# A causal cross-attention and expert layer on one core: the order of the attention step, with one slot of single products per step instead of two

## The chip, the core and the metric

The kernel runs on one core of one Trainium2 chip. A core has a matrix engine (TensorE, PE in the profile; its weight loads are the row PEld), a vector engine (VectorE, DVE), a scalar engine (ScalarE, ACT), a general engine (GpSimd, POOL) and a queue that issues transfers (SyncE, SP). Each engine works through its own list of instructions in order and waits on semaphores that the others raise. Products land in PSUM, from where DVE and ACT read them; everything else is in SBUF or in HBM (DRAM).

The metric is the time of one execution in microseconds (us) of device time, lower is better. Where several runs were taken, their median is given.

## The reference

Everything is float32. Four sequences of 1024 tokens with 512 features pass through an attention layer and a layer of experts, both with a residual.

```python
# attention, 16 heads of 32
qh, kh = (ln(x) @ Wq.T), (ctx @ Wk.T)          # by head
vh = ctx @ Wv.T + bv
scores = einsum('bhsd,bhtd->bhst', qh, kh) / sqrt(32)
mask = triu(ones((1024, 1024)), k=0); mask[0, 0] = False
probs = softmax(where(mask, -inf, scores))
x = x + (einsum('bhst,bhtd->bhsd', probs, vh)) @ Wo.T + bo
# experts: in each group of 32 tokens every one of 128 experts takes the token with its largest logit
perm = (logits == max over the 32 tokens of logits)
x = x + combine(relu(dispatch(ln(x), perm) @ f1 + bias) @ f2, perm)
```

Row s of the scores uses keys before s only (row 0 its own key), so about half of every 1024x1024 block is computed. The attention is what the change is about; the routing and expert phases come after it and their code is not touched.

## The kernel before, in words

**Units and steps.** The attention is cut into 16 units: 4 sequences times 4 chunks of four heads. A unit has 12 steps (k = 0 to 11), and every engine's list is written out by hand in the order of the Python loop (only the transfers on SP are placed by the scheduler of the framework).

In a step of unit u, three attention products are made, each for four heads at once:

- `score_piece(u+1, k)` makes row-major scores of the *next* unit: 128 queries against up to 512 keys (L401, four matmuls that use 32 rows of the array each and run side by side), for 8 of the 12 steps followed by a product that adds the causal mask (L407, full array). DVE takes the row maxima from PSUM, one instruction for two heads (L413). The widths for k = 0 to 11 are 128, 256, 384, 512, 512, 128, 512, 256, 512, 384, 512, 512; pieces 4, 6, 8 and 10 have no mask.
- `key_block(u, k)` makes key-major scores of *this* unit: 128 keys against up to 512 queries (L467), and subtracts the row maxima, which were made one unit before, by a second product (L473). ACT takes the exponential from PSUM (L481), and POOL zeroes the masked part on the diagonal (L484). The widths are 512, 384, 256, 128, 512, 512, 512, 512, 512, 384, 256, 128.
- `weigh_values(u, k)` multiplies the exponentials of block k with the values (L517, four matmuls that use 32 columns of the array each, side by side). It is put on a list, `pending`, and made when the list holds LAG = 2, so two steps after its block.

The sums of the exponentials are added up by POOL and DVE (L500 to L504); at the end of each half of a unit `normalize` makes their totals on PE (L543), takes reciprocals and multiplies the result (L538).

**Three PSUM buffers for two kinds of scores.** Pieces and blocks take two buffers each from one pool of three (`ps_s`, each of two banks). Since they alternate, the first half of a block takes the buffer that the block before had for its second half, and the second half takes the one that the piece before had for its first half; pieces likewise. So a block's second half can't start before DVE has read the first half of the piece ahead of it, and a piece's second half not before ACT has read the first half of the block ahead of it.

**Single products.** Between these come the products that prepare later units or finish earlier ones: queries (L288), keys (L274), values (L307), output rows (L348), and the small turn of the row maxima (L439, "pmx"). They use the full array and one PSUM bank (`ps_m`), so a second one waits until ACT or DVE has emptied the bank of the first. They stand in lists (`fill`, `soon`), and `slot(slots_left, until)` takes from them: it works towards a backlog that falls evenly over the slots left, and further while the planner's clock `now` is before `until`. `ensure` forces those that are needed next. A product is cut into four parts of one 512-wide matmul (a value product into four of four 128-wide ones), so a slot can stop in the middle.

**The planner's clock.** `now`, `dve`, `act` and `bank` hold the author's estimates of when each engine is done; `scores_free()` says when both halves of the next pair of score buffers are free. These estimates decide the order only; nothing of them is in the program.

Before the change, a step reads (L716 to L763): piece; a slot until the score buffers are free; the value product if they are still not free; block; sums; the value product if it was not made; a second slot.

Of the kernel before, what the change touches and what calls it, by code (L numbers as in the profile page):

```python
# [37 lines left out]
def attention_phase(  # L38
# [20 lines left out]
    NU = B * NC  # L59

    LARGE, SMALL, TURN = 0.86, 0.11, 0.2
    now, dve, act, bank = [0.0], [0.0], [0.0], [0.0]

    read = deque([0.0] * 3)
# [5 lines left out]
    def scores_free():  # L72
        return max(read[0], read[1]) + 0.1

    def scores_given(work, engine, cost):
        now[0] = max(now[0], scores_free()) + work
        for _ in range(2):
            read.popleft()
            read.append(given(engine, cost))
# [308 lines left out]
    def score_piece(u, k):  # L388
        i, c0, n = pieces[k]
        kT, qT = ks[u], qs[u]  # L390
        half = i // 4
        if (u, half) not in nms:
            nms[u, half] = spool.tile([P, 2, 4, R], F32, tag=f"nm{half}", name=f"nm_{u}_{half}")
        nm = nms[u, half]
        scs = [
            ps_s.tile([P, 2, HS], F32, tag="sc", name=f"sc_{u}_{k}_{g}") for g in range(2)
        ]
        diag = c0 + n == (i + 1) * P
        for r in range(R):
            rr = ds(r * HD, HD)  # L400
            nc.tensor.matmul(  # L401
                scs[r // 2][:, r % 2, :n], lhsT=qT[rr, ts(i, P)], rhs=kT[rr, ds(c0, n)],
                start=True, stop=not diag,
            )
        if diag:
            for r in range(R):
                nc.tensor.matmul(  # L407
                    scs[r // 2][:, r % 2, ds(n - P, P)], lhsT=ident16,
                    rhs=masks[0 if i == 0 else 1], start=False, stop=True,
                )  # L410
        scores_given(LARGE * n / HS + (0.45 if diag else 0.1), dve, 0.15 + 2.1e-3 * n)
        for g in range(2):
            nc.vector.tensor_reduce(  # L413
                nm[:, c0 // HS, i % 4, ts(g, 2)], scs[g][:, :, :n], AX.X, ALU.max, negate=True
            )
# [166 lines left out]

    fill, soon, done = deque(), deque(), set()
    open_step, backlog = [None], [0.0]
    RESERVE = 5.0
# [20 lines left out]
    def choose(force):  # L608
        for i in range(len(soon)):
            if soon[i][0] <= now[0] or (force and not fill):  # L610
                step = soon[i][1]
                del soon[i]
                return step
        return fill.popleft() if fill else None

    def slot(slots_left, until=0.0):

        goal = backlog[0] - max(0.0, backlog[0] - RESERVE) / slots_left
        if backlog[0] > goal or now[0] < until:
            now[0] += TURN  # L620
        while backlog[0] > goal or now[0] < until:
            if open_step[0] is None:
                if now[0] < bank[0]:
                    return
                open_step[0] = choose(False)
                if open_step[0] is None:
                    return
            if not advance(open_step[0]):
                open_step[0] = None
# [20 lines left out]
    def ensure(*names):  # L650
        while not done.issuperset(names):
            one_part()
# [27 lines left out]
    def o_todo(b, t0, t1):  # L680
        return [o_step(b, t, ahead=(b, t + 1) if t + 1 < NT else None) for t in range(t0, t1)]
# [5 lines left out]
    STEPS = len(blocks)  # L687
    LAG = 2
    pending, sums = deque(), deque()
    for half in range(2):  # L690
        done.update((kind, 0, half) for kind in "qkv")
    for u in range(-1, NU):
        b, hc = divmod(u, NC)
        q_todo, k_todo = kq_steps(u + 2) if u + 2 < NU else ([], [])
        v_todo = v_steps(u + 1) if 0 < u + 1 < NU else []
        more = 0 <= b < B - 1

        rows, r0 = [], 0
        if b > 0:
            if hc == 0:  # L700
                load_residual(b - 1, 0)
            ends = (3, 6, 8, 8) if more else (2, 4, 7, 8)
            r0 = ends[hc - 1] if hc else 0
            rows = o_todo(b - 1, r0, ends[hc])
        if more and hc == 0:
            ln_rows(b + 1)
        add("q", u + 2, q_todo[:1] if more and hc == 2 else q_todo)
        if more and hc == 1:
            load_ctx(b + 1, 0)
            add("t", b + 1, [ln_step_turned(b + 1)], 0.0)  # L710
        add("v", u + 1, v_todo)
        if more and hc == 2:
            add("c", b + 1, [load_step(b + 1, 1)], 0.0)
            add("k", u + 2, k_todo[:1])
            add("o", b - 1, rows, first=r0)
            add("k", u + 2, k_todo[1:], first=1)  # L716
            add("q", u + 2, q_todo[1:], first=1)
        else:
            add("k", u + 2, k_todo)
            add("o", b - 1, rows, first=r0)  # L720
        for k in range(STEPS):
            if u + 1 < NU:
                if k in (0, 4):
                    ensure(("q", u + 1, k // 4), ("k", u + 1, k // 4))
                score_piece(u + 1, k)
                if k == 4:
                    split_maxima(u + 1, 0)
                if k == STEPS - 1:
                    split_maxima(u + 1, 1)
            weighed = False  # L730
            slot(2 * (STEPS - k), scores_free() if u >= 0 else 0.0)
            if u >= 0 and len(pending) == LAG and now[0] < scores_free():
                pending.popleft()()
                weighed = True
            if u >= 0:
                h, j = blocks[k]
                finish(("split", u, h, 0), ("split", u, h, 1))
                while (u, h) not in mxTs:
                    one_part()
                key_block(u, k)  # L740
            if sums:
                sums.popleft()()
            beside(0.9)
            if len(pending) == LAG and not weighed:
                pending.popleft()()
            if u >= 0:

                def add_first(u=u, k=k):
                    add_sums(u, k, 0, nc.vector)

                def weigh(u=u, k=k):
                    h, j = blocks[k]
                    ensure(("v", u, j // 4))
                    weigh_values(u, k)
                    if j == 4 * (h + 1) - 1:
                        if h == 0 and NC <= u and u % NC == NC - 1:
                            ensure(("o", u // NC - 1, NT - 1))
                        soon.append((now[0], normalize(u, h)))

                add_sums(u, k, 1, nc.gpsimd)  # L760
                sums.append(add_first)
                pending.append(weigh)
            slot(2 * (STEPS - k) - 1, scores_free() if u + 1 < NU else 0.0)  # L763
    while sums:
        sums.popleft()()
    while pending:
# [396 lines left out]
```

## Time and profile before

| | us |
|---|---|
| median of 3 runs | 1498.17 |
| runs | 1489.71, 1498.17, 1499.57 |
| the profiled execution's own time | 1487.66 |
| its span, from first to last instruction | 1485.9 |
| PE busy in the span | 1400.1 |
| DVE busy | 926.8 |
| ACT busy | 502.7 |
| POOL busy | 486.4 |
| mean granted clock of PE | 0.972 of full |

The profile shows one execution. A group of instructions is named by its line in the kernel, its engine, and `out<-in` by tile names: `sc` is a piece of row-major scores, `st` a block of key-major scores, `av` the value product, `pr` the exponentials, `pq`, `pk`, `pv`, `po` the single products. A float32 matmul makes two passes through the array, and each pass is one record: a group of four matmuls shows as x8. Ends of matmuls are modelled, starts are recorded, so what a group takes is read here from its start to the start of the next group. The attention steps fill the span from 39.9 us (first piece) to 1138.3 us (last value product); the routing and expert phases follow.

### The profile page before, as it was taken

How to read it: one execution, taken by the hardware profiler on the slowest of the kernel's cores; microseconds unless marked ns; L12 is line 12 of the kernel's file. 1: busy time of each engine (PE TensorE's matmuls, PEld its weight loads, DVE VectorE, ACT ScalarE, POOL GpSimd, SP SyncE). 2: the span in 40 equal slices, each digit the busy share in tenths (PEclk: the TensorE clock that was granted, in tenths of full speed). 3: DMA queues.
4: the chain of work that ended last, by engine and by line, in shares of the span. 5: the costliest groups of instructions: out<-in, count | busy, mean ns of one | idle time of the engine just before them, and what ended most of it. 6: DMA issues, size and time to landing. Idle time of an engine off the chain costs nothing.

```text
span 1485.9 us, 31726 instructions
## 1 busy us (share of the span) xinstructions
PE 1400.1 (94%) x13704; PEld 739.5 (50%) x13704; DVE 926.8 (62%) x1377; ACT 502.7 (34%) x785; POOL 486.4 (33%) x557
## 2 busy tenths in 40 slices
PE   6999999999899999999999999999997988968996
PEld 4344544354344534443434344444533547868886
DVE  3666777565657676666767755655754554756664
ACT  1033333423232233232323233232333124636662
POOL 1034334343334343435253443434366200000212
PEclk9999999999999999999999999999997996988999
DMA  8011201002231300012211100010113788652654
GB/s 298 21 50 32 76 24 66 20 1 59 38 111 36 96 29 19 10 52 47 72 60 50 33 11 10 10 38 19 38 47 122 268 273 241 191 193 79 207 181 143
DMA packets 96972, 125.25 MB, mean 84 GB/s; under 512 B 12992, under 2 KB 54336, under 8 KB 96704
## 3 DMA queue, kind: packets, MB, share of 16 engines
q1 hardware_dynamic: 94272, 114.84, 24.9%
q0 software_dynamic: 2560, 8.39, 1.9%
q8 instruction: 107, 1.75, 0.5%
q14 instruction: 33, 0.27, 0.1%
HBM read 91.78 MB, written 31.42 MB: 83 GB/s over the span
## 4 chain that ended last, share of the span: by engine, by line
PE 78%; issue 7%; DVE 5%; DMA 5%; POOL 2%; ACT 1%; SPq 0%; POOLq 0%; DVEq 0%; ACTq 0%
PE sc L401 12%; PE st L467 10%; PE av L517 8%; PE pq L288 8%; PE pk L274 8%; PE pv L307 8%; PE po L348 5%; PE pd L957 3%; PE sc L407 3%; DVE nm L413 2%; PE pi L976 2%; PE st L473 2%; PE po L808 2%; PE pl L845 2%; PE pd L543 2%
## 5 line engine op out<-in xcount | busy, mean ns | idle before, releaser
L413 DVE TENSOR_REDUCE nm<-sc 128x2 f32<-128x1024 f32 (+3 forms) x384 | 349.1, 951 | 265.3 <-PE sc L407 178.9
L481 ACT ACTIVATE pr<-st 128x1024 f32<-128x1024 f32 (+3 forms) x384 | 290.4, 808 | 583.9 <-PE st L473 557.6
L484 POOL TENSOR_SCALAR_AFFINE_SELECT pr<-pr 128x256 f32<-128x256 f32 x256 | 122.5, 488 | 383.0 <-ACT pr L481 380.9
L504 POOL TENSOR_TENSOR acc<-acc,pr 128x1024 f32<-128x1024 f32 (+3 forms) x128 | 209.2, 1634 | 93.3 <-ACT pr L481 85.6
L401 PE MATMUL sc<-kT,qT 32*128 32x512 f32 (+3 forms) x1536 | 206.3, 531 | 8.6 <-ACT pr L481 4.9
L467 PE MATMUL st<-qT,kT 32*128 32x512 f32 (+3 forms) x1536 | 191.1, 534 | 4.6 <-DVE nm L413 4.5
L517 PE MATMUL av<-pr,v 128*32 128x512 f32 (+3 forms) x1536 | 166.2, 501 | 8.0 <-POOL pr L484 4.3
L274 PE MATMUL pk<-ct,w_k 128*128 128x512 f32 x256 | 131.0, 629 | 10.0 <-DMA w_k<-in_wkT_dram 9.2
L307 PEld LDWEIGHTS pv<-w_v,ct 128*128 128x128 f32 x1024 | 119.5, 192 | 34.6 <-issue 25.6
L504 DVE TENSOR_TENSOR acc<-acc,pr 128x1024 f32<-128x1024 f32 (+3 forms) x128 | 126.5, 989 | 9.2 <-POOL pr L484 9.0
L467 PEld LDWEIGHTS st<-qT,kT 32*128 32x128 f32 x1536 | 68.6, 183 | 127.5 <-issue 99.8
L401 PEld LDWEIGHTS sc<-kT,qT 32*128 32x128 f32 x1536 | 74.4, 183 | 115.4 <-issue 50.6
L307 PE MATMUL pv<-w_v,ct 128*128 128x128 f32 x1024 | 131.4, 281 | 0.2 <-DMA w_v<-in_wvT_dram 0.2
L288 PE MATMUL pq<-xnT,w_q 128*128 128x512 f32 x256 | 127.3, 616 | 1.5 <-ACT xnT L194 1.5
L501 POOL TENSOR_TENSOR acc<-pr,pr 128x768 f32<-128x768 f32 (+1 forms) x32 | 66.8, 2086 | 161.4 <-ACT pr L481 161.4
L1074 POOL DMA_DIRECT2D out_dram<-xr x32 | 24.2, 757 | 259.2 <-DVE xr L1073 258.8
L348 PE MATMUL po<-w_o,atT 128*128 128x512 f32 x192 | 95.5, 616 | 0.0
L517 PEld LDWEIGHTS av<-pr,v 128*32 128x32 f32 x1536 | 32.1, 108 | 94.9 <-issue 67.2
L274 PEld LDWEIGHTS pk<-ct,w_k 128*128 128x128 f32 x256 | 43.9, 194 | 69.0 <-issue 54.2
L473 PE MATMUL st<-mxT,ones 32*128 32x512 bf16 (+3 forms) x768 | 74.6, 322 | 0.3 <-DVE mxT L444 0.3
L288 PEld LDWEIGHTS pq<-xnT,w_q 128*128 128x128 f32 x256 | 43.0, 189 | 52.9 <-issue 46.2
L1058 PE MATMUL pt<-ident,y 128*128 128x128 f32 x512 | 58.3, 277 | 5.3 <-DVE y L1033 4.6
(101 smaller groups left out, 1495.2 us busy)
## 6 DMA issues: line engine op xcount, KB each, us to landing
ct<-in_ctxT_dram SPq DMA_DIRECT2D x8, 1024.0 KB, 5.1
xt<-in_x_dram SPq DMA_DIRECT2D x8, 1024.0 KB, 5.8
xr<-in_x_dram SPq DMA_DIRECT2D x32, 256.0 KB, 2.7
xn_dram<-x SPq DMA_DIRECT2D x8, 1024.0 KB, 4.8
xn<-xn_dram SPq DMA_DIRECT2D x8, 1024.0 KB, 5.8
f<-in_f_dram SPq DMA_DIRECT2D x16, 512.0 KB, 4.1
xr<-x_dram SPq DMA_DIRECT2D x32, 256.0 KB, 4.1
f<-in_f_dram SPq DMA_DIRECT2D x32, 256.0 KB, 4.3
```

What stands on the lines that cost most here:

```text
L274: nc.tensor.matmul(pk, lhsT=weights["k"][:, c, ts(hc, P)], rhs=cts[b, half][:, c, :], start=(c == 0), stop=(c == NC - 1),)
L288: nc.tensor.matmul(pq, lhsT=weights["q"][:, c, ts(hc, P)], rhs=xnTs[b][:, c, ts(half, HS)], start=(c == 0), stop=(c == NC - 1),)
L307: nc.tensor.matmul(pv[:, t, :], lhsT=cts[b, half][:, c, ts(t, P)], rhs=weights["v"][:, c, ts(hc, P)], start=(c == 0), stop=(c == NC - 1),)
L348: nc.tensor.matmul(po, lhsT=atTs[b * NC + c][:, ts(t, P)], rhs=weights["o"][:, c, :], start=(c == 0), stop=(c == NC - 1),)
L401: nc.tensor.matmul(scs[r // 2][:, r % 2, :n], lhsT=qT[rr, ts(i, P)], rhs=kT[rr, ds(c0, n)], start=True, stop=not diag,)
L413: nc.vector.tensor_reduce(nm[:, c0 // HS, i % 4, ts(g, 2)], scs[g][:, :, :n], AX.X, ALU.max, negate=True)
L467: nc.tensor.matmul(scs[r // 2][:, r % 2, :n], lhsT=kT[rr, ts(j, P)], rhs=qT[rr, ds(h * HS + q0, n)], start=True, stop=False,)
L473: nc.tensor.matmul(scs[r // 2][:, r % 2, :n], lhsT=ones16[rr, :], rhs=mxT[rr, ds(q0, n)], start=False, stop=True,)
L481: nc.scalar.activation(pr[:, :, :n], scs[g][:, :, :n], AF.Exp)
L484: nc.gpsimd.affine_select(out=d, in_=d, compare_op=ALU.is_ge, fill=0.0, base=0 if j == 0 else -1, pattern=[[0, 2], [P + 1, P]], channel_mu ...
L504: engine.tensor_tensor(acc, acc, pr[:, :, :n], ALU.add)
L517: nc.tensor.matmul(avs[u, h][rr, q0:], lhsT=vs[u][:, j, rr], rhs=pr[r // 2][:, r % 2, : HS - q0], start=(j == 0), stop=(j == last),)
```

## The change

The step is written in another order: block, value product, (a slot only if the planner's clock is more than SHORT = 0.5 before the score buffers come free), piece, sums, one slot. The value product always comes straight behind the block. The one slot at the end of the step works towards a backlog spread over half as many slots, and, while there are blocks, fills until the buffers are free. The same products are made, with the same tiles and buffers; `score_piece`, `key_block`, `weigh_values`, `slot` and the single products are not changed.

```diff
+    SHORT = 0.5
...
         for k in range(STEPS):
-            if u + 1 < NU:
-                if k in (0, 4):
-                    ensure(("q", u + 1, k // 4), ("k", u + 1, k // 4))
-                score_piece(u + 1, k)
-                if k == 4:
-                    split_maxima(u + 1, 0)
-                if k == STEPS - 1:
-                    split_maxima(u + 1, 1)
-            weighed = False
-            slot(2 * (STEPS - k), scores_free() if u >= 0 else 0.0)
-            if u >= 0 and len(pending) == LAG and now[0] < scores_free():
-                pending.popleft()()
-                weighed = True
             if u >= 0:
                 h, j = blocks[k]
                 finish(("split", u, h, 0), ("split", u, h, 1))
                 while (u, h) not in mxTs:
                     one_part()
                 key_block(u, k)
+            if len(pending) == LAG:
+                pending.popleft()()
+            if u + 1 < NU:
+                if k in (0, 4):
+                    ensure(("q", u + 1, k // 4), ("k", u + 1, k // 4))
+                if now[0] + SHORT < scores_free():
+                    slot(2 * (STEPS - k), scores_free())
+                score_piece(u + 1, k)
+                if k == 4:
+                    split_maxima(u + 1, 0)
+                if k == STEPS - 1:
+                    split_maxima(u + 1, 1)
             if sums:
                 sums.popleft()()
             beside(0.9)
-            if len(pending) == LAG and not weighed:
-                pending.popleft()()
...
-            slot(2 * (STEPS - k) - 1, scores_free() if u + 1 < NU else 0.0)
+            slot(STEPS - k, scores_free() if u >= 0 else 0.0)
```

## The prediction

> **What bounds the kernel now.** I read the page first: shares of engines, then the chain that ended last.
>
> ```profile
> span 1485.9 us, 31726 instructions
> PE 1400.1 (94%) x13704; PEld 739.5 (50%) x13704; DVE 926.8 (62%) x1377; ACT 502.7 (34%) x785; POOL 486.4 (33%) x557
> PE 78%; issue 7%; DVE 5%; DMA 5%; POOL 2%; ACT 1%; SPq 0%; POOLq 0%; DVEq 0%; ACTq 0%
> ```
>
> PE is the bound. Busy time per stretch says the same of the attention steps: in 500 to 600 us PE is busy 98.98 of 100 us, DVE 68.41, at the full granted clock (columns: stretch, PE, PEld, DVE, ACT, POOL, clock, DMA share, GB/s):
>
> ```profile
> 500.00:600.00 100.00, 98.98 (x818) 45.16 (x816) 68.41 (x96) 32.78 (x43) 37.80 (x34) 1.00 0.14 42
> ```
>
> But "busy" hides two things, which the timeline of PE shows (start, duration, instruction):
>
> ```profile
> 36.31 3.70 PE L288 MATMUL pq<-xnT,w_q 128*128 128x512 f32 x8 [0.74 <-ACT xnT L194]
> 39.94 0.39 PE L401 MATMUL sc<-kT,qT 32*128 32x128 f32 x4
> ...
> 415.61 0.29 PE L473 MATMUL st<-mxT,ones 32*128 32x256 bf16 x4
> 415.72 1.98 PE L401 MATMUL sc<-kT,qT 32*128 32x512 f32 x8
> 417.64 0.40 PE L407 MATMUL sc<-mask_strict,ident 128*128 128x128 bf16 x4
> ...
> 421.01 1.98 PE L288 MATMUL pq<-xnT,w_q 128*128 128x512 f32 x4
> 422.92 1.14 PE L401 MATMUL sc<-kT,qT 32*128 32x512 f32 x8
> 423.99 3.70 PE L288 MATMUL pq<-xnT,w_q 128*128 128x512 f32 x8
> ```
>
> First, **turns**. Eight passes of a product take 39.94 - 36.31 = 3.63 us until the next group, four take 422.92 - 421.01 = 1.91. So a pass is 0.43 us and each uninterrupted run of single products has a fixed 0.2 us on top: about 0.09 where the array goes from one layout (32 rows, full, 32 columns) to another, and 0.10 more for the first pass. Second, **held halves**. The piece at 422.92 takes 1.07 us; the one at 415.72, of the same width, takes 1.92, because it stands straight behind a block and its second half waits until ACT has read that block. Both look busy.
>
> Taking each group of the attention steps (39.9 to 1138.3 us, 1098.4 us) in this way, from start to start: 851 us are passes, 163 us turns, 84 us are held halves and waits. Of the 84: pieces 40 (piece 7 alone 16, piece 3 10), blocks 28 (6.6 of it one wait for a transfer), value products 5, single products 10.
>
> **The change, turns.** The built instruction order gives the counts: runs of single products fall from 317 to 219, layout changes from 880 to 814. A run costs 0.15 us behind a mask product (same layout) and 0.20 elsewhere; pieces cost 0.21 to 0.23 so, blocks 0.22, value products 0.14. Summed by kind over each order: 163 us before, 148 after, **-15 us**, on PE's own path, with nothing to hide behind. The other pace of the one slot, and the 0.5 us that SHORT lets stand, act through these counts and the waits below.
>
> **The change, held halves.** Rows that set them:
>
> ```profile
> L481 ACT ACTIVATE pr<-st 128x1024 f32<-128x1024 f32 x192 | 186.1, 1021 | 310.6 <-PE st L473 285.1 <-POOL acc L504 25.5
> ...
> L413 DVE TENSOR_REDUCE nm<-sc 128x2 f32<-128x1024 f32 x192 | 225.8, 1217 | 141.2 <-PE sc L401 85.6 <-PE sc L407 55.0
> ...
> L413 DVE TENSOR_REDUCE nm<-sc 128x2 f32<-128x256 f32 x64 | 23.9, 415 | 40.1 <-PE sc L407 40.1
> ```
>
> Counted from the start of the group behind a block, ACT's first half is read after 1.15 us for width 512 (start-up, then 1.02), 0.91, 0.69 and 0.48 for 384, 256, 128; PE goes on 0.05 later. A value product takes 1.00, 0.78, 0.57, 0.35 us for the same widths. Its block is two steps older, so the pairs by step are fixed:
>
> *Pieces*, now behind block and value product. Steps 6, 7, 8 (512 against 512): 1.20 - 1.00 = 0.20, 15 units each, 45 x 0.20 = 9.0; but 21 of these blocks were themselves held, so that ACT starts early: less 4.2. Steps 2, 3, 9, 10, 11: covered, nothing. Steps 0, 1, 4, 5 have a short value product behind a long block (up to 0.85 short), and there the new slot stands: in the order a run is there 50 times in all; without one: step 4 five times, 1.20 - 0.57 = 0.64; step 5 three times, 0.85; step 1 seven times only the short turn of the maxima, 0.28. Together 3.2 + 2.6 + 2.0. Sum 12.6, and 4 for the first pieces, which have no blocks (as now): 17 against 40.
>
> *Blocks*, behind a piece. With no run between, the wait is DVE's first half: 0.48, 0.74, 1.00 and 1.27 us for widths 128, 256, 384 and 512 with mask, 1.38 without (so the 415 and 1217 ns above, and start-up). The new order has this 33 times: 12 at step 6, 8 at steps 0 and 1, 6 at step 2, 3 at step 5, 4 elsewhere. Step 6: 12 x 0.48 = 5.8; step 1: 7 x 0.48 = 3.4; step 2: 6 x 0.74 = 4.4; step 5: 3 x 1.38 = 4.1; the five others 5.9: 23.6. Behind the short turn alone (0.33 of cover) 19 times, 9 of them at step 8 (0.41), the rest 0.4 to 1.05: 12.6. Behind one part of a product at step 7: 1.0. A half held longer than a pass costs 0.10 more, as at 415.72: 42 x 0.10 = 4.2. Sum 41, and the last unit as now 6: 47 against 28. This is what the change gives back: before, only one block stood straight behind a piece. Behind a held half stand, on PE, the value product and the next piece, which is why it is counted in full; ACT and POOL wait for the block too, but are busy 33 and 38 of 100 us.
>
> *The rest*: value products 5 as now; single products hand over their one bank inside a run about 10 times at 0.85 us, 10 in all, as now. The transfer:
>
> ```profile
> 372.73 0.69 DVE L538 TENSOR_TENSOR atT<-raw,inverse 128x512 f32<-128x512 f32 x1 [7.57 <-DMA inverse<-inverse_dram]
> ...
> 375.40 1.22 PE L467 MATMUL st<-qT,kT 32*128 32x512 f32 x2 [4.29 <-DVE nm L413]
> ```
>
> DVE stood 7.57 us on `inverse`, which was queued on SP behind a load of statistics not yet written; the block's second half and all behind it waited. In the new order of SP that load no longer stands ahead of this one, but others moved (statistics of the next sequence now come later, behind other stores); bounds 0 and 8, I take 3, nearer to nothing since the only wait of this size is the one whose cause goes. Of the moved steps' own transfers (`inverse`, `xr`, `both`, `xnT`, `ct`) none is new; the multiplication by `inverse` stays two steps behind its request, as now. DVE and POOL do the same instructions.
>
> Sum of waits: 17 + 47 + 5 + 10 + 3 = 82 against 84, **-2**. With the turns -17; and since the two-halves arithmetic, put to the old order, came out 0.1 to 0.3 us high where the block ahead had been held itself (step 7: 0.98 worked out, 0.68 to 0.75 measured), and 52 blocks are now held, I take off another 3: **-20 us**. The routing and expert phases don't change. Against its own execution that is 1487.7 - 20 = 1468; that execution stood 10.5 us below the median of the runs, 1498.2, so the forecast for a median is **1478**.
>
> **A rule against it.** The Trainium skill (TensorEngine Tiling (Array Packing), "PSUM Bottleneck") warns that tiling speeds up TensorE but not the emptying of PSUM. A full piece is 0.86 us of passes but 2 x 1.217 = 2.43 on DVE. If emptying were the bound, the runs between would be free cover and taking one away would cost its whole cover: 52 bare blocks at about 1.3 us are 68 us, and the change would lose 7 us (68 in place of the 41 above). By the rows, the bare places are mostly behind narrow pieces (415 and 685 ns), and DVE is busy 68 of 100; so 41.
>
> **Rivals.** *A, as worked out*: 1478. *B, the waits only move*: if DVE reaches the maxima 0.3 us later than now at the 52 bare blocks (16 us), the turns are eaten: 1478 + 16 = 1494. For it: DVE's sums take 1484 ns at full width when POOL works beside it, and two steps without a run follow each other at steps 1 to 2 and 5 to 6. Against: those have the narrow pieces. *C, slower: DVE's queue becomes the bound in the bare steps.* A full step without runs is 1.07 + 1.29 + 1.00 = 3.4 us on PE; DVE has 2.43 of maxima, 1.48 of sums and up to 0.95 of something else, 4.9. Late by 1 us at the 52, that is 52 us on A: 1530. It passes zero at 20 / 52 = 0.4 us and is over 1% at 0.7. Against: runs of 3.4 us (whole products) follow at steps 0, 3, 9, 10, 11 and let DVE catch up. *D, the slots don't disappear*: the planner could fill as often as before; then 1498. The order (219 runs) excludes that. A waiting chain on SP like the above, with PE idle for more than about 3 us, would also halve the clock for a while (TensorE: Matmul & The Clock Gate, "Why this matters for your kernels"); the wait of 4.29 shows it, as the same product took 0.64 us at 377 instead of 0.39. None of the waits summed above is longer than 1.4, so I add nothing.
>
> **Numbers.** A 0.54, B 0.28, C 0.18. A covers 1455 (bare blocks at half price, no transfer wait: -43) to 1483, B 1484 to 1508, C above. Faster by over 1% (below 1483), which is about what can be told from no change, 0.54; within 1% 0.29; slower by over 1% 0.17. A range of 1455 to 1508 leaves out the most of C.
>
> **What would show it.** In the profile of the changed kernel: the span of the attention steps falls from 1098 to about 1078; piece 7 takes about 1.1 us (0.43 of passes, 0.45 of turns and mask, 0.20 held) where it now takes 1.3 to 1.9; blocks at steps 1, 2, 6 and 8 show their second half 0.4 to 0.7 us late; PE's starts behind products keep the 0.2. I am wrong if blocks behind bare pieces are held by 1 us or more on average (C), if DVE's idle time before the maxima falls far below its present 265 us with PE's waits rising, or if a wait on a transfer of several us stands in the chain.

## The result and the profile after

In 20 runs each, taken together, the changed kernel took 1503.16 us (median; 1493.95 to 1518.2) and the kernel before 1496.48 (1485.18 to 1501.68): a ratio of 1.0062, 95% interval 1.0036 to 1.0087. (The ratio leaves out one run of the changed kernel, at 1518.2, which was in a slower state; the medians alone stand 6.7 us, or 0.45%, apart.) The change costs about 0.6%, where a gain of 20 us was forecast. The time lies inside the forecast's range; sign and size were wrong.

The page of the changed kernel. All its line numbers from the attention code are 2 higher than before.

```profile
span 1496.8 us, 31702 instructions
PE 1402.0 (94%) x13704; PEld 746.0 (50%) x13704; DVE 918.0 (61%) x1377; ACT 501.8 (34%) x785; POOL 479.5 (32%) x557
```

The shares look as before; a stretch of 100 us in the middle (same columns as in the prediction) has PE at 98.32 in place of 98.98:

```profile
500.00:600.00 100.00, 98.32 (x788) 44.33 (x781) 66.82 (x93) 32.42 (x43) 39.29 (x37) 0.99 0.13 42
```

So the loss has to be found as the prediction found it: from each group's start to the start of the next, less its passes and its turn of the array. What is left is waiting. (Passes are taken at full speed, so a lower clock is in the waits too; and a wait at the start of a group is booked on the group ahead of it.) The last column is the part that sits in single waits of more than 2 us.

| attention steps, us | length | passes | turns | waits | pieces | blocks | value products | single products | over 2 us |
|---|---|---|---|---|---|---|---|---|---|
| before | 1098.4 | 851.4 | 163.1 | 83.7 | 43.4 | 27.3 | 5.1 | 8.0 | 11.7 |
| forecast of the change | about 1078 | 851 | 148 | 79 | 17 | 47 | 5 | 10 | 3 of a transfer |
| after | 1109.5 | 851.8 | 148.0 | 109.5 | 29.7 | 53.5 | 7.8 | 18.5 | 26.0 |

The rest of the span is 387.5 us before and 387.3 after. The turns fell by the 15 us that were forecast. The waits rose by 25.8 instead of falling, and 14.3 of that are eight waits above 2 us where there were three. One kind of them had no counterpart before. PE's timeline (start, duration, instruction; in brackets the time that its engine stood, and who released it), at a place that comes twice:

```profile
493.03 0.40 PE L409 MATMUL sc<-mask_strict,ident 128*128 128x128 bf16 x4
493.26 0.39 PE L441 MATMUL pmx<-ident,mxs 128*128 128x128 bf16 x4
493.58 2.18 PE L469 MATMUL st<-qT,kT 32*128 32x512 f32 x8
497.49 0.40 PE L475 MATMUL st<-mxT,ones 32*128 32x512 bf16 x4 [1.73 <-DVE mxT L446]
497.81 1.08 PE L519 MATMUL av<-pr,v 128*32 128x256 f32 x8
498.83 2.30 PE L403 MATMUL sc<-kT,qT 32*128 32x512 f32 x8
```

and DVE's timeline at the same time:

```profile
493.35 2.35 DVE L415 TENSOR_REDUCE nm<-sc 128x2 f32<-128x1024 f32 x2 [0.88 <-PE sc L409]
495.62 0.68 DVE L506 TENSOR_TENSOR acc<-acc,pr 128x512 f32<-128x512 f32 x1
496.22 0.69 DVE L338 BATCH_NORM_STATS2 row_stats<-xr 128x6 f32<-128x512 f32 x1
496.94 0.18 DVE L339 BATCH_NORM_AGGREGATE moments<-row_stats 128x2 f32<-128x6 f32 x1
497.04 0.39 DVE L446 COPY mxT<-pmx 128x512 bf16<-128x512 bf16 x1
```

The turn of the row maxima (pmx) ends at 493.6, but its copy stands in DVE's queue behind piece 3's maxima, a sum and a row statistic, and runs at 497.04. Block 4 subtracts these maxima, so it loses 2.94 us. For 1.73 of them PE stands idle for the copy; most of the rest is its second half, which waits for the maxima of piece 3 and which the forecast had counted (1.27 less 0.33 of cover, 0.94). The piece behind starts at half the clock. It stays so for 3.41 us, while a wait of 2.87 us at 669.76 left the clock full (columns as in the prediction):

```profile
497.83:501.24 3.41, 3.41 (x21) 1.10 (x18) 0.29 (x1) 1.94 (x2) 0.00 (x0) 0.50 0.27 77
669.80:673.40 3.60, 3.60 (x9) 1.41 (x10) 3.56 (x5) 0.00 (x0) 0.00 (x0) 1.00 0.07 25
```

In the attention steps after, the clock stands at 0.50 in six stretches, in which PE is busy for 23.8 us; before, in three, with 10.5. At half the clock half of that time is lost, so by this estimate 11.9 us against 5.2: about 6.7 of the 25.8 us of new waits are passes at half the clock.

In the groups, the late copy is the idle time of L475, which is 0.3 before (L473). That of L403 comes from keys that were made only just ahead of the piece that needs them; there it is mostly ACT's copy itself that PE waits for (0.59 us, six times). The last two lines are the maxima, before (L413) and after (L415):

```profile
L473 PE MATMUL st<-mxT,ones 32*128 32x512 bf16 (+3 forms) x768 | 74.6, 322 | 0.3 <-DVE mxT L444 0.3
L475 PE MATMUL st<-mxT,ones 32*128 32x512 bf16 (+3 forms) x768 | 85.0, 323 | 5.3 <-DVE mxT L446 5.3
L403 PE MATMUL sc<-kT,qT 32*128 32x512 f32 (+3 forms) x1536 | 196.0, 543 | 7.8 <-ACT kT L281 5.4 <-ACT pr L483 2.4
L413 DVE TENSOR_REDUCE nm<-sc 128x2 f32<-128x1024 f32 (+3 forms) x384 | 349.1, 951 | 265.3 <-PE sc L407 178.9 <-PE sc L401 85.6
L415 DVE TENSOR_REDUCE nm<-sc 128x2 f32<-128x1024 f32 (+3 forms) x384 | 348.6, 949 | 312.6 <-PE sc L409 196.7 <-PE sc L403 115.4
```

They speak against a DVE that has too much to do: its idle time ahead of the maxima rose from 265.3 to 312.6 us. Two more of the eight are DVE standing on a transfer in front of work that PE needs: 4.14 us at 106, and 3.06 us at 665.6, in DVE's timeline

```profile
668.22 0.69 DVE L213 BATCH_NORM_STATS2 ln_stats<-xt 128x6 f32<-128x512 f32 x1 [4.56 <-DMA xt<-in_x_dram]
```

and in PE's, whose one bank is emptied by the instruction L315 that stands behind these statistics:

```profile
669.76 3.70 PE L276 MATMUL pk<-ct,w_k 128*128 128x512 f32 x8 [2.87 <-DVE v L315]
```

By cause, the eight waits above 2 us are: transfers 7.2 us (before 6.6), the maxima's turn 5.9 (before none), the last unit, where value products wait for POOL and nothing is left to put between, 8.0 (before 5.1), block 9 at 1081.8 with four small steps of DVE ahead of its maxima 2.4, and 2.5 at 727.7 whose cause I did not settle.

### The profile page after: what moved, and what is told of

Read it like the earlier page. It is cut to its first block, busy times and chain, and to the rows that moved or that the text cites. A ratio compares the mean times of both kernels' runs of the same rounds, so it can differ in the third digit from the quotient of the medians.

```text
span 1496.8 us, 31702 instructions
## 1 busy us (share of the span) xinstructions
PE 1402.0 (94%) x13704; PEld 746.0 (50%) x13704; DVE 918.0 (61%) x1377; ACT 501.8 (34%) x785; POOL 479.5 (32%) x557
## 4 chain that ended last, share of the span: by engine, by line
PE 79%; issue 7%; DVE 6%; DMA 4%; POOL 2%; ACT 1%; SPq 0%; POOLq 0%; DVEq 0%; ACTq 0%
PE sc L403 11%; PE st L469 11%; PE av L519 9%; PE pv L309 8%; PE pk L276 7%; PE pq L290 7%; PE po L350 6%; PE pd L957 3%; PE sc L409 3%; DVE nm L415 2%; PE st L475 2%; PE pi L976 2%; PE po L808 2%; PE pl L845 2%; PE pd L545 2%
## 5 line engine op out<-in xcount | busy, mean ns | idle before, releaser
L415 DVE TENSOR_REDUCE nm<-sc 128x2 f32<-128x1024 f32 (+3 forms) x384 | 348.6, 949 | 312.6 <-PE sc L409 196.7
L486 POOL TENSOR_SCALAR_AFFINE_SELECT pr<-pr 128x256 f32<-128x256 f32 x256 | 117.6, 467 | 376.2 <-ACT pr L483 373.4
L469 PE MATMUL st<-qT,kT 32*128 32x512 f32 (+3 forms) x1536 | 215.3, 534 | 7.3 <-DVE nm L415 6.4
L403 PE MATMUL sc<-kT,qT 32*128 32x512 f32 (+3 forms) x1536 | 196.0, 543 | 7.8 <-ACT kT L281 5.4
L403 PEld LDWEIGHTS sc<-kT,qT 32*128 32x128 f32 x1536 | 71.0, 185 | 144.9 <-issue 84.1
L506 DVE TENSOR_TENSOR acc<-acc,pr 128x1024 f32<-128x1024 f32 (+3 forms) x128 | 133.1, 1040 | 6.7 <-POOL pr L486 6.6
L276 PE MATMUL pk<-ct,w_k 128*128 128x512 f32 x256 | 122.8, 614 | 12.6 <-DMA w_k<-in_wkT_dram 9.2
L469 PEld LDWEIGHTS st<-qT,kT 32*128 32x128 f32 x1536 | 77.3, 183 | 108.8 <-issue 67.5
L309 PE MATMUL pv<-w_v,ct 128*128 128x128 f32 x1024 | 123.5, 278 | 0.0
L350 PE MATMUL po<-w_o,atT 128*128 128x512 f32 x192 | 91.2, 608 | 0.8 <-DVE xr L356 0.8
L475 PE MATMUL st<-mxT,ones 32*128 32x512 bf16 (+3 forms) x768 | 85.0, 323 | 5.3 <-DVE mxT L446 5.3
```

Of the source, the lines that this page charges most:

```text
L276: nc.tensor.matmul(pk, lhsT=weights["k"][:, c, ts(hc, P)], rhs=cts[b, half][:, c, :], start=(c == 0), stop=(c == NC - 1),)
L309: nc.tensor.matmul(pv[:, t, :], lhsT=cts[b, half][:, c, ts(t, P)], rhs=weights["v"][:, c, ts(hc, P)], start=(c == 0), stop=(c == NC - 1),)
L350: nc.tensor.matmul(po, lhsT=atTs[b * NC + c][:, ts(t, P)], rhs=weights["o"][:, c, :], start=(c == 0), stop=(c == NC - 1),)
L403: nc.tensor.matmul(scs[r // 2][:, r % 2, :n], lhsT=qT[rr, ts(i, P)], rhs=kT[rr, ds(c0, n)], start=True, stop=not diag,)
L415: nc.vector.tensor_reduce(nm[:, c0 // HS, i % 4, ts(g, 2)], scs[g][:, :, :n], AX.X, ALU.max, negate=True)
L469: nc.tensor.matmul(scs[r // 2][:, r % 2, :n], lhsT=kT[rr, ts(j, P)], rhs=qT[rr, ds(h * HS + q0, n)], start=True, stop=False,)
```

## The experiments

**Theory 1, "just in time".** With one slot a step and its pace, single products whose results are needed soon are made at the last moment. The result then has to pass through DVE's or ACT's queue behind what already stands there, and PE waits. **Theory 2** is the forecast's case C: DVE has too much work in the steps without a run. **Theory 3**: fewer slots leave blocks without cover ("bare": no single products between a piece and the block behind it), which is the whole loss.

### The turn of the maxima two groups of a step earlier

```diff
             if len(pending) == LAG:
                 pending.popleft()()
+            if u >= 0 and k == 2:
+                finish(("split", u, 1, 0), ("split", u, 1, 1))
+                while (u, 1) not in mxTs:
+                    one_part()
```

> The changed kernel, but at step 2 of each unit the rest of the second half's row maxima is split and turned before piece 2, so that no turn of maxima stands straight before block 4. Theory 1, just in time (the paced slot leaves single products to the last moment, and what comes last is then waited for on DVE or ACT): in the changed kernel block 4 waits 10.3 us in all and the piece 4 behind it 4.5; they should fall to about 4 together, turns of the array go up by 1.5 us (228 runs of single products in the order in place of 219), so the time falls by 8 to 10 us against the changed kernel's 1503, to about 1494, and is within 0.3% of the kernel before. Theory 2, DVE's queue is late: the maxima's turn only moves two steps forward in the same queue, the waits come back at blocks 2 and 3, the time stays within 3 us of 1503. Theory 3, blocks without a run ahead of them are what costs: nothing changes at those, the time stays at 1503 plus the turns.

1491.7 us, 0.9962 of the kernel before (0.9944 to 0.998): 11 us better than the changed kernel, and ahead of the kernel before. Block 4 waits 4.6 instead of 10.3, piece 4 0.5 instead of 4.6, all waits 96.9 instead of 109.5. In the groups the wait on the copy is gone and that on keys is not:

```profile
L475 PE MATMUL st<-mxT,ones 32*128 32x512 bf16 (+3 forms) x768 | 85.8, 323 | 0.0
L403 PE MATMUL sc<-kT,qT 32*128 32x512 f32 (+3 forms) x1536 | 190.3, 537 | 6.4 <-ACT kT L281 5.4 <-ACT pr L483 1.0
```

About 10 of the 11 us are at block 4 and piece 4, where the edit aims. (A run of single products now covers most blocks 4, so the held half goes with the late copy.) Theory 1 forecast the place and the amount; theory 2 had the waits come back at blocks 2 and 3, and they did not (3.9 us together there, before the edit 5.8); theory 3 saw nothing to gain.

### Keys and queries one step earlier

```diff
             beside(0.9)
+            if k == 3 and u + 1 < NU:
+                ensure(("q", u + 1, 1), ("k", u + 1, 1))
+            if k == STEPS - 1 and u + 2 < NU:
+                ensure(("q", u + 2, 0), ("k", u + 2, 0))
```

> The changed kernel, but the keys and queries that pieces 4 and 0 need are finished one step earlier (at the end of steps 3 and 11, behind the value product). Theory 1: the waits of first pieces for the copy of their keys by ACT (5.8 us at six pieces 0 in the changed kernel) go, and nothing comes in their place: 5 us less than the changed kernel's 1503, about 1498. Theory 2 and theory 3: the copy by ACT plays no part, the waits move to the blocks behind, within 2 us of 1503.

1507.89 us, 1.0085 (1.0058 to 1.0111): every theory missed. The waits on ACT's copy of the keys did go (L403's idle time fell to 3.3 us, none of it on kT), but waits above 2 us rose from 26.0 to 43.6. The copy of the maxima is late three times now, and at 225 DVE stands on a transfer in front of the maxima of a bare block. DVE's timeline:

```profile
226.72 0.98 DVE L540 TENSOR_TENSOR atT<-raw,inverse 128x512 f32<-128x512 f32 x1 [3.12 <-DMA inverse<-inverse_dram]
```

and PE's, the second half of block 6, which waits 5.0 us in all:

```profile
228.91 1.10 PE L469 MATMUL st<-qT,kT 32*128 32x512 f32 x2 [2.90 <-DVE nm L415]
```

Moving products moves all later slots of the plan, and DVE's side work with them.

### Both edits

> Both edits in the changed kernel: maxima of the second half turned at step 2, keys and queries finished a step earlier. Theory 1: the gains add, 12 to 14 us less than the changed kernel's 1503, about 1490, ratio to the kernel before 0.993 to 0.998; the waits of the attention steps fall from 109.5 to about 97 us and the turns rise from 148 to 149.5. Theory 2: what is taken from block 4 and piece 0 comes back at the other blocks, ratio 1.004 to 1.008 as the changed kernel has it. Theory 3: the same, 1.005.

1481.42 us, 0.9907 (0.9874 to 0.9939): 0.9% faster than the kernel before and 1.5% faster than the changed one, more than expected. Waits fall from 109.5 to 87.8, those above 2 us from 26.0 to 13.0, turns are 149.4. Both copies that PE waited for have left the groups:

```profile
L403 PE MATMUL sc<-kT,qT 32*128 32x512 f32 (+3 forms) x1536 | 190.2, 538 | 0.7 <-ACT pr L483 0.7
L475 PE MATMUL st<-mxT,ones 32*128 32x512 bf16 (+3 forms) x768 | 86.1, 322 | 0.0
```

It still has 33 bare blocks, as the changed kernel has (28.7 us of waits there against 26.9). So bare blocks are a price that the change can pay. About 15 of the 21.7 us of waits that are gone were where the edits aim, half of them at block 4 and piece 4 and half at the single products. The rest went with the plan: the waits at 665.6 and 727.7 are not there in this order, which no theory foresaw.

### Two slots in the new order

```diff
-                if now[0] + SHORT < scores_free():
-                    slot(2 * (STEPS - k), scores_free())
+                slot(2 * (STEPS - k), scores_free() if u >= 0 else 0.0)
...
-            slot(STEPS - k, scores_free() if u >= 0 else 0.0)
+            slot(2 * (STEPS - k) - 1, scores_free() if u >= 0 else 0.0)
```

> The changed kernel's order of a step (block, value product, piece), but with two slots of single products a step at the old paces and without the tolerance of 0.5 us; the order has 302 runs of single products in place of 219. Turns of the array are 160.7 us by their counts, 12.6 more than in the changed kernel. Theory 1: the waits at block 4 and at first pieces need not fall, since the pace leaves the maxima late also here (6 of 7 turns of maxima still stand straight before block 4), while blocks without a run ahead come back (39 in the order): time 1503 plus 5 to plus 13. Theory 3 (fewer slots are what exposes the blocks): waits fall to the 84 us of the kernel before, time 1503 - 25 + 13 = 1491.

1546.86 us, 1.0353 (1.0304 to 1.0401): far worse than either. Theory 3 falls: with more slots the waits are 143.0 us, not 84. (This order has 39 bare blocks, so it does not tell what one costs.) Theory 1 named the sign but not the size. Twelve bare blocks stand behind the full piece 6 without a mask, which cost 1.58 us each, 18.9 in all. This is one of them: 1.50 us from the first half to the second, where 0.43 is a pass.

```profile
456.48 1.02 PE L469 MATMUL st<-qT,kT 32*128 32x512 f32 x4
457.98 0.70 PE L469 MATMUL st<-qT,kT 32*128 32x512 f32 x2 [0.47 <-DVE nm L415]
```

Block 4 waits 15.3 us, and waits above 2 us add up to 56.1, among them 7.6 and 8.0 us while DVE stands on the transfer of `inverse`. These two are waits for a transfer, not for cover.

### No tolerance in the one slot

```diff
-    SHORT = 0.5
+    SHORT = 0.0
```

> The changed kernel with the tolerance SHORT at 0 in place of 0.5 us, so that a slot is filled whenever the planner counts any wait for the buffers of a piece: 264 runs of single products in the order in place of 219, turns 156.9 us in place of 148.1. Theory 3 (bare blocks and short waits are what the tolerance lets stand): waits fall by more than the 9 us that the turns add, time below 1503. Theory 1: the turns of maxima straight before block 4 stay (6 of 7), first pieces as well (16 of 17): time 1503 plus 3 to plus 9.

1531.24 us, 1.0249 (1.0189 to 1.031). Turns are 156.8, as counted; the waits did not fall but rose to 143.2, with 48.3 above 2 us. Theory 3 is wrong again, and theory 1's sum is too small by some 20 us.

### Less work for DVE, in both kernels

```diff
-            engine.tensor_tensor(acc, acc, pr[:, :, :n], ALU.add)
+            if engine is nc.vector:
+                engine.tensor_tensor(acc[:, :, :16], acc[:, :, :16], pr[:, :, :16], ALU.add)
+            else:
+                engine.tensor_tensor(acc, acc, pr[:, :, :n], ALU.add)
```

Both kernels then leave out most of DVE's half of the sums.

> The changed kernel with DVE's running sums of the weights narrowed to 16 columns for all blocks but the first two of a half (leaves out the most of DVE's half of the sums; POOL's half stays), so that DVE loses about 1.3 us of work in most steps. Theory 2, DVE's queue is the bound in the bare steps: the 25.8 us of new waits go for the most part, 20 us or more less than the changed kernel. Theory 1: blocks behind a piece wait for the maxima of that piece, which DVE reads as early as now (it stands 313 us idle before them); only the copies of turned maxima and keys that stand behind a sum come sooner: 3 to 8 us less than the changed kernel, and the kernel before gains a like amount by the same edit. Theory 3: no change, within 2 us.

> The same narrowing of DVE's sums in the kernel before (leaves out the same part). Theory 1: 2 to 6 us less than the kernel before, so that the distance between the two kernels stays within 4 us of the 9 us that it is. Theory 2: the kernel before does not wait for DVE's queue at the places that the change made bare, it gains 5 us less than the changed kernel by this edit or still less, and the distance shrinks by 15 us or more.

In the changed kernel 1490.18 us, 0.9964 (0.9944 to 0.9985); in the kernel before 1487.12, 0.9943 (0.9926 to 0.9959). The distance between the two shrinks from 0.62% to 0.21%, about 6 us (3.6 by the medians), where each of the two distances is uncertain by some 4 us: about the 4 us that theory 1 allowed, or a little more, and less than the 15 of theory 2. By the traces the attention waits fall by 7.4 us (109.5 to 102.1) and by 4.4 (83.7 to 79.3), so that the gap between the two kernels' waits goes from 25.8 to 22.8 us. DVE's load may have a part in it, 3 us by the traces and 4 to 6 by the times; it is not what the change lost most of its gain to.

### The value product behind its block, in the kernel before

```diff
             slot(2 * (STEPS - k), scores_free() if u >= 0 else 0.0)
-            if u >= 0 and len(pending) == LAG and now[0] < scores_free():
-                pending.popleft()()
-                weighed = True
```

> The kernel before with one edit: a value product always comes behind its step's block, never ahead of it; slots as before. This is the part of the change that the forecast credits with the pieces (16 us at piece 7 and 10 at piece 3), without its thinner slots. If the arithmetic of the held halves is right, the pieces behind blocks lose their waits (9 places in the order where a block is directly followed by a piece were 24, now none) and blocks behind pieces without a run rise from 1 to 41 in the order: pieces 40.6 to about 20, blocks 28 to 45, turns unchanged at 163: within 8 us of the kernel before on either side. Theory 3 predicts it as slow as the changed kernel and the turns: 1503 + 15.

1515.8 us, 1.0139 (1.0085 to 1.0194). The pieces gained even more than the arithmetic said, from 43.4 to 10.3 us, but blocks went from 27.3 to 81.5, where 45 had been expected: 25 us at step 6, where most blocks stand straight behind the full piece 6 at 1.58 us each; 10.9 at step 7; and two waits of 7.5 and 7.9 us at block 8 with DVE on the transfer of `inverse`. So the held pieces that the forecast went after are worth having only if the blocks are not left bare by the same move.

### The same two edits in the kernel before

> The kernel before (old order, two slots) with the same two edits that made the changed kernel 22 us faster: maxima of the second half turned at step 2, keys and queries finished one step earlier. Theory 1: with two slots these products were seldom late, so there is little to gain: the waits at block 4 (1 to 2 us) and for keys (2.2 us) go, the turns rise by 1.9 (165.1): 1494 to 1500, the same as the kernel before, and the thinner slots are then worth 13 to 18 us once their late products are made in time. Rival: the edits help any order alike, the kernel before gains 10 us or more (1486 or less), and the thinner slots are worth nothing.

1511.88 us, 1.0093 (1.0069 to 1.0117). The edits do not help any order: there they cost 14 us, more than theory 1 thought. Forced products now follow each other in one run, and single products wait 23.8 us instead of 8.0, on each other's bank (9.5 us) and on reciprocals of DVE. With these edits in both, the new order with one slot is 30 us ahead.

### Filling the bare place at step 5

```diff
+            at = parts[0]
             slot(STEPS - k, scores_free() if u >= 0 else 0.0)
+            if k == 4 and u >= 0 and parts[0] == at:
+                for _ in range(2):
+                    if open_step[0] or fill or soon:
+                        one_part()
```

(`parts` counts calls of `advance`; on top of both edits.)

> The changed kernel with both edits, and with two parts of a single product at the end of step 4 wherever the planner leaves that place empty, so that block 5 no longer stands straight behind the full piece 4. In the trace those bare blocks wait 1.58 us each, 6.6 in all. In the order, bare blocks at step 5 fall from 4 to 0, at step 2 from 8 to 4, at step 6 from 13 to 11, and 8 come up at step 10 and 2 at step 8, since the parts are missing later; turns rise from 149.5 to 152.3. Theory 1 with the price per bare place (1.58 at step 5, 0.73 at step 2, 0.55 at step 6, 1.05 at step 10): -6.6 -2.9 -1.1 +8.4 +1 = about -1, with the turns +2: time 1479 to 1487, no gain. Theory 3 (a bare block costs the same wherever it is): 29 in place of 33 of them, 4 us less waits, 1480; the two differ in where the waits are seen: blocks 10 at 8 us or more in the trace by theory 1.

1528.03 us, 1.0205 (1.0172 to 1.0237): no theory came near. The local step did what it should: blocks 5 wait 0.9 us instead of 6.6. Elsewhere waits above 2 us rose from 13.0 to 45.9. Block 10 has two of 4.86 us. DVE's timeline at the first:

```profile
387.31 1.76 DVE L540 TENSOR_TENSOR atT<-raw,inverse 128x512 f32<-128x512 f32 x1 [1.43 <-DMA inverse<-inverse_dram]
...
389.81 0.39 DVE L446 COPY mxT<-pmx 128x512 bf16<-128x512 bf16 x1
390.11 1.81 DVE L415 TENSOR_REDUCE nm<-sc 128x2 f32<-128x768 f32 x2
```

PE's, and busy time in the stretch at the lower clock (columns as in the prediction):

```profile
391.12 0.80 PE L469 MATMUL st<-qT,kT 32*128 32x256 f32 x2 [3.55 <-DVE nm L415]
392.49 1.94 PE L519 MATMUL av<-pr,v 128*32 128x512 f32 x8
```

```profile
389.42:396.25 6.83, 5.13 (x24) 1.37 (x24) 4.39 (x8) 1.09 (x2) 0.81 (x2) 0.50 0.00 0
```

A multiplication that waits for its transfer, statistics and a copy stand ahead of piece 9's maxima. The block's second half stands 3.55 us, and the value product behind it takes 1.94 us in place of 1.06, at a granted clock of 0.50 for 6.83 us. Another pair, 6.5 and 6.4 us, is a query product that waits for DVE to normalise its input.

### The multiplication two steps further behind its transfer

```diff
+            if name[0] == "pause":
+                budget -= 0.9
...
             later(("wait", u, h), 0.9, lambda: None, front=True)
+            for i in range(2):
+                aside.appendleft(("pause", u, h, i))
```

> The changed kernel with both edits, and the multiplication by the inverse sums two steps further behind the request of its transfer. In the changed kernel DVE stands 5 us on that transfer at 107 us, because the request is queued on SP behind a load of statistics whose store has not landed, and PE's block 8 waits 3.9 to 5.0 us for DVE. If this is so, that wait of 3.8 us goes; the planner shifts its other steps a little (turns 149.4 in place of 149.5, 30 bare blocks in place of 33, but 7 of them at step 11): time 1474 to 1480, where the two edits alone give 1481. If the wait is not the transfer's, the block at about 106 us still waits 3 us or more.

1559.09 us, 1.041 (1.038 to 1.0439). The wait at block 8 did go: nothing above 0.25 us is left between 98 and 116. But the pauses hold up the whole list of DVE's side work, which is then forced at once in front of something else. The largest case: four statistics that wait for their rows stand ahead of piece 10's maxima, and block 11 waits 9.2 us. DVE's timeline:

```profile
784.95 0.69 DVE L215 BATCH_NORM_STATS2 ln_stats<-xt 128x6 f32<-128x512 f32 x1 [5.05 <-DMA xt<-in_x_dram]
```

and PE's:

```profile
790.23 0.58 PE L471 MATMUL st<-qT,kT 32*128 32x128 f32 x2 [8.37 <-DVE nm L417]
```

The expectation blamed the queue of SP. In the trace of both edits that holds for the most of it: the reciprocals were ready at 95.3, and SP sent them at 100.1, 4.8 us later, after it had stood 9.5 us on a store of statistics; the store of the reciprocals itself then took 4.9 us more. I did not take the load on SP away alone, since the scheduler places SP's transfers.

### The turn of the maxima one group earlier only

The edit of the first experiment, with `k == 3` for `k == 2`.

> The changed kernel, with the turn of the second half's maxima moved by one group only: from behind piece 3 to just ahead of it (the earlier run moved it ahead of piece 2 and gained 11 us). Its copy then stands ahead of piece 3's maxima in DVE's queue, but nothing stands between piece 3 and block 4 any more: in the order 41 blocks are bare in place of 33, the new ones at step 4, where a bare block waits 1.26 us. Theory 1 with the queue's order as the cause: the 2.94 us waits on the copy go, 7 bare blocks at 1.26 (8.8) come in the place of 8.1 us there, and only the piece 4 behind them gains (4.6 to about 1): 3 us less than the changed kernel, about 1500; the earlier run's gain needs both, the copy early and a run of single products left as cover. Rival, lateness in time alone: the copy is early enough, the gain is that of the earlier run, about 1492.

1516.6 us, 1.0129 (1.0111 to 1.0147): worse than both said. Block 4 and piece 4 gained 12 us (10.3 to 2.2 and 4.6 to 0.9), more than by theory 1. What it does not count is where the parts that cover block 4 now come from: blocks 5 are bare seven times (11.1 us in place of 4.7), and block 10 waits 4.95 us twice with a multiplication and a normalisation of DVE ahead of its maxima. DVE's timeline:

```profile
530.75 2.17 DVE L242 TENSOR_TENSOR xnT<-xnT,both 128x512 f32<-128x512 f32 x1
```

and PE's:

```profile
534.17 0.80 PE L469 MATMUL st<-qT,kT 32*128 32x256 f32 x2 [3.64 <-DVE nm L415]
```

### All together

| | time, us | turns | waits | of these over 2 us |
|---|---|---|---|---|
| before | 1496.5 | 163.1 | 83.7 | 11.7 |
| after | 1503.2 | 148.0 | 109.5 | 26.0 |
| turn at step 2 | 1491.7 | 149.5 | 96.9 | 13.6 |
| keys earlier | 1507.9 | 147.0 | 118.6 | 43.6 |
| both | 1481.4 | 149.4 | 87.8 | 13.0 |
| two slots | 1546.9 | 160.6 | 143.0 | 56.1 |
| no tolerance | 1531.2 | 156.8 | 143.2 | 48.3 |
| value product late, before | 1515.8 | 163.4 | 109.0 | 25.4 |
| both, before | 1511.9 | 165.0 | 104.3 | 11.6 |
| both, step 5 filled | 1528.0 | 152.2 | 134.0 | 45.9 |
| both, multiplication later | 1559.1 | 149.3 | 168.9 | 78.2 |
| turn at step 3 | 1516.6 | 148.1 | 123.2 | 31.4 |

(The two kernels that leave out sums are not in the table.) The times span 78 us. With the last column taken off, they span 36 (1464 to 1500). So a good half of what sets these orders apart is a handful of long waits, most of them on DVE's queue.

Theory 1 is weak as a forecast of times: the first run came within 3 us of its figure and the two with narrowed sums within 5; the other nine missed theirs by 9 to 79 us. Every edit that moves products shifts the whole plan, so a total time alone is no evidence for a cause here; what counts is whether the waits go at the place that an edit aims at.

## Why the prediction was wrong

**Turns: right.** -15 us by the counts, -15.1 in the trace.

**Bare blocks: right in their regular part.** The price by width of the piece, worked out as 0.48, 0.74 and 1.38 us at steps 1, 2 and 5, and 0.48 at step 6, measured 0.46, 0.73, 1.58 and 0.55. Blocks came to 53.5 us against 47 and 3 for a transfer.

**"Single products hand over their one bank ... 10 in all, as now": this step failed.** It took the waits of products and of their readers from the old order. Measured: single products 18.5 us, of which 5.8 is keys made just ahead of their piece, where nothing had been counted, and about 7 the bank. The same failed assumption is in the blocks: "behind the short turn alone" was costed as cover for block 4 (0.33 us), and nobody asked what the turn's own copy has to wait for. The blocks 4 behind the turn wait 8.1 us, where the forecast had about 1.9 (0.94 for each of the two that follow the turn alone).

**Pieces: 29.7 us against 17.** Piece 7 fell from 16 to 3.7 us as said. Of the 12.7 us that are missing, 3.1 are the piece 9 at 665.6, behind which the bank stood on a transfer, 2.5 the one at 727.7, and 1.4 the pieces 4 (4.6 where 3.2 had been counted); the rest is small and spread over the other steps.

**"None of the waits summed above is longer than 1.4, so I add nothing": wrong in its conclusion.** There were eight above 2 us, with 26.0 us between them. The one transfer that was watched did go, and two others came (7.2 us in place of 3). The last unit, put "as now", grew too: 8.0 us of long waits in place of 5.1. The limit was wrong as well: the forecast, by the page that it cites, saw the clock fall where PE is idle for more than about 3 us, but at 497.49 it fell behind 1.73 us of idle time, so the lower clock had to be counted (about 6.7 us more than before, by the estimate above).

**The 3 us taken off at the end: not borne out.** Piece 7, put at 15 x 0.20 = 3.0 us before this deduction, measured 3.7.

**The rivals.** D is out by the order and by the turns. C is out as the main cause: DVE stood idle for longer, and narrowing its sums took only 3 to 6 us more from the changed kernel than from the one before. B, "the waits only move", put 1494 on a DVE that comes to the maxima 0.3 us late everywhere; the result is nearer to it, but by another mechanism: pieces whose first half is read more than 0.5 us late because DVE is still at other work fell from 23 to 7. None of the cases was the one that happened: a product needed at once, with its copy still to be made, and for the maxima behind other work in the queue of an engine that is busy 61% of the time.

What is shown: that in this order the late turn of the maxima costs about 10 us at its place (taken away alone, 11 us in all), and that with the late keys taken away as well the changed order is 22 us faster than it was and 0.9% faster than the kernel before. What is only argued: that the keys alone are worth the other half, since alone they gained nothing, and some 6 us of that half are waits that left with the plan. What stays open: the cause of the 2.5 us at 727.7, and which of DVE's side steps meets which transfer in a given order.

## What to carry to other kernels

When slots for filler work are made fewer, list for each filler who needs its result, and what stands ahead of its copy in the reader's queue when it comes at the last moment: for the maxima the cost was the queue (up to 3 us), not the copy (0.4). An engine with plenty of idle time can hold up the bound engine all the same, if a step of its side work waits for a transfer in front of what PE needs. Costs by place add up only while the order of the other engines stays put; after an edit that shifts the plan, look for the single waits above 2 us first.

## What the runs showed of the hardware

After a long wait PE can be slower for a while: behind the 3.55 us wait above, a value product took 1.94 us instead of 1.06 and the piece after it 2.06 where it stands at 1.14 elsewhere, at a clock of 0.50. So the wait cost 1.8 us more in these two alone. The length of the wait alone does not decide it: behind 1.73 us of idle PE (497.49) the clock was halved for 3.41 us, and behind 2.87 us (669.76) it was not.

A small instruction on DVE can take ten times its usual time while POOL works: a subtraction of 16 columns took 1.92 us beside a sum on POOL, where 0.18 is usual, and held up what stood behind it. In the trace of the changed kernel this subtraction (L434) starts beside a sum of POOL five times; each time it took 1.66 to 1.92 us and ended within 0.05 us of POOL's sum. DVE's and then POOL's timeline:

```profile
725.07 1.92 DVE L434 TENSOR_TENSOR rest<-rest,mxs 128x16 f32<-128x16 f32 x1
```

```profile
724.59 2.36 POOL L503 TENSOR_TENSOR acc<-pr,pr 128x1024 f32<-128x1024 f32 x1 [7.64 <-ACT pr L483]
```

A store of 4 KB of statistics took about 10 us until what waited for it could go on (88.70 to 98.7). The load of 1 MB that was sent 1.5 us ahead of it landed after 5.2 us; how much of the ten is owed to that load is not shown.
